# The last four steps of a two-level Winograd graph kernel, finished product by product and in pieces of 128 features

## The chip, the cores and the metric

The kernel runs on one core of one Trainium2 chip. The metric is device microseconds of one execution, the median of a few runs. Engines are named as in the profile: PE (TensorE matmul) and PEld (its weight loads), DVE (VectorE), ACT (ScalarE), POOL (GpSimd), SP (SyncE, which issues DMAs here). Places in time are microseconds from the start of the profiled span.

## What is computed

Two graph layers over N = 4096 nodes with D = 512 features, all float32:

```python
# layer 0: inc = adj + (adj > 0) / row norm of that mask
x1  = layernorm(x + (inc @ x) / rowsum(inc))
# layer 1: A2 = adj + I, dscale = diag(A2) ** -0.5
temp = A2 @ x1 @ W.T
out  = layernorm(x1 + relu((dscale[:, None] * A2 * dscale[None, :]) @ temp))
```

The three 4096 x 4096 products are what costs time. The change touches the last of them and the relu, the addition of x1 and the layernorm behind it.

## The kernel before

**Tiling.** Each product is done with Winograd's form of Strassen's method, seven products in place of eight, at two levels in layer 1. The outer level gives seven operand pairs p (1 to 7); the inner level gives, for each pair, seven matmuls. `steps` (L189) lists the work of layer 1: k is 2 for A2 @ x1 and 3 for the normalised product, s (0, 1) a half of the output nodes, p in the order of ORDER (L179), kk (0 to 7) a slice of the contraction. A step is seven matmuls of 128x512 into seven PSUM banks, one for each inner product (`multiply2`, L272 to L278); the banks collect the eight kk of one (k, s, p). bank(7) is the spare one (`spare`), used for transposes. Features lie on partitions in these results, nodes along the free dimension.

**Operands of a step.** `load` fetches a tile `a` of adjacency (four quarters of 512 columns). `prepare` adds the identity where the diagonal lies (`complete`, L174) and forms four sums S3, S1, S2, S4 with DVE in `add_up`: L167 (two sums, 1024 wide), L169 (S2), L170 (S4). `sum_b` (L257 to L259) does the same for the other operand, once for two steps. Steps are prepared LA = 2 ahead.

**After a group of eight steps** `outer` decodes the seven banks into quarter tiles C (`inner`, L684 to L692): quarter 0 is q1+q2; with u2 = q6+q1 and u3 = q7+u2 quarter 1 is q3+(u2+q5), quarter 2 is q4-u3, and quarter 3 is -u3-q5. They are added to or subtracted from what lies in C (L695, L699, L913).

**Rows of the result.** When a half of C is done for some nodes, `layer1` (L859) takes a block of 128 nodes: four 128x128 transposes on PE (L844) into the spare bank, `rectify` on ACT (L848: relu with scale), and in `rest`, one step later, `add` of x1 on DVE (L695), bn_stats (L149), bn_aggr (L151), sqrt on ACT (L153), `normalise` (L159 and L161 on DVE, L162 on ACT) and a store issued by POOL (L873). x1 comes back from DRAM with `fetch` (L857, POOL queue). Sixteen blocks of s = 0 and eight of s = 1 go this way, one or two beside each step.

**The last eight blocks** (h = 1, s = 1) need the very last group, k = 3, s = 1, p = 4. Their second halves of features (H = 256 wide) are done early by `layer1_first`: two blocks at a time, two transposes each into bank 7, rectify into o[:, H:D], x1 added by POOL (L887), bn_stats (L892). These are taken up from `queue` beside the steps of the last group, two for each of its steps as long as there are any. In the last group three layer1 blocks and then four layer1_first pairs remain, so the fourth pair comes by itself at step kk = 4.

**The end.** The last TAIL = 3 steps (kk = 5, 6, 7) are prepared but not multiplied in the loop. `finish` (L895 on) does them product by product, all three steps of q1, then of q2, q6, q5, q3, q7, q4 (L908), so that quarters are decoded while later products run. c21 holds four quarters of 128 features by 512 nodes: c21[:, 0] and c21[:, 1] belong to blocks 0 to 3 (r = 0), c21[:, 2] and c21[:, 3] to blocks 4 to 7 (r = 1). `put` (L910 to L913) makes a quarter in two DVE operations: the sum into a temporary y, then y - c21. `turn(t)` transposes both quarters' columns of block t into a bank of its own, rectifies 256 features, and adds x1 on POOL (L922). `measure(t)` is bn_stats, bn_aggr, sqrt (L927, L929, L931); `leave(t)` normalises on ACT or, in one tensor_scalar, on DVE (L940, L941), and stores through SP (L942). The order is written out by hand:

```python
        multiply(q7)
        for t in range(4):
            turn(t)
        ... u3, put(3) ...
        multiply(q4)
        measure(0); measure(1)
        put(2, ...)
        for t in range(4, 8):
            turn(t)
        ... measure and leave, alternating ...
```

**What sets the order.** The scheduler is off (`manual_schedule`): every engine runs its instructions in the order in which the program issues them, and waits on semaphores. So an instruction that waits holds all that stands behind it on its engine, DMA issues on POOL and SP included.

Of the kernel before, what the change touches and what calls it, by code (L numbers as in the profile page):

```python
# [8 lines left out]
F32 = mybir.dt.float32  # L9
# [4 lines left out]
P = 128  # L14
# [12 lines left out]
def tile_adj_resnorm_d2(  # L27
# [148 lines left out]

    TAIL = 3
    LA = 2
# [49 lines left out]
    def prepare(n):  # L228
        k, s, p, kk = steps[n]
        for i in range(n, len(steps) if n == len(steps) - TAIL else n + 1):  # L230
            complete(i)
# [8 lines left out]
        made["s"] += 1  # L240
        sm = (work, pools["work"], work)[i % 3].tile([P, 4, SW], F32, tag="s", name="s")
        add_up(sm, a)
# [616 lines left out]
    def layer1(h, item):  # L859

        j, r, cols = item
        b = j + h * NP
        y = late.pop(b)
        o = late["pool"].tile([P, D], F32, name="o", bufs=4)
        ps = spare()
        turn_back(ps, 0, h, r, cols, (0, 1))
        rectify(o, ps, b)

        def rest():
            add(o, y)  # L870
            mv, sd = statistics([o])
            normalise(o, mv, sd)
            nc.gpsimd.dma_start(out=out[b * P:(b + 1) * P, :], in_=o)  # L873
        later.append(rest)

    def layer1_first(h, *items):
# [4 lines left out]
        for i, (j, r, cols) in enumerate(items):  # L881
            b = j + h * NP
            o = late["pool"].tile([P, D], F32, name=f"o{b}")
            st = late["pool"].tile([P, 2, 6], F32, name=f"st{b}")
            rectify(o[:, H:D], ps[:, i * H:(i + 1) * H], b)
# [3 lines left out]
        def rest():  # L889
            for j, _, _ in items:  # L890
                _, o, st = late[j + h * NP]
                nc.vector.bn_stats(st[:, 1, :], o[:, H:D])  # L892
        later.append(rest)

    def finish(h, items, acc):  # L895


        c21 = C_of[3][h][0]
        q1, q2, q6, q5, q7, q3, q4 = range(7)
        p1, p5, u2, u3 = (row_tile(t, 1) for t in ("p1", "p5", "u2", "u3"))  # L900
        w2 = row_tile("t", 1, (P, 4, H))[:, 0:2, :].rearrange("p a d -> p (a d)")
        tail = [(steps[n][3], factors(n)) for n in range(len(steps) - TAIL, len(steps))]
        stats = {}

        def multiply(m):
            for kk, f in tail:
                right, left = f[m]
                nc.tensor.matmul(acc[m], left, right, start=False, stop=(kk == NQ - 1))  # L908

        def put(i, op):  # L910
            y = row_tile("y", 2)
            op(y)
            nc.vector.tensor_sub(c21[:, i, :], y, c21[:, i, :])  # L913

        def turn(t):
            j, r, cols = items[t]
            b = j + h * NP
            ps = bank((t + 7) % 8)
            turn_back(ps, 0, h, r, cols, (0,))
            y, o, _ = late[b]  # L920
            rectify(o[:, 0:H], ps[:, 0:H], b)
            nc.gpsimd.tensor_add(o[:, 0:H], o[:, 0:H], y[:, 0:H])  # L922

        def measure(t):
            b = items[t][0] + h * NP
            _, o, st = late[b]
            nc.vector.bn_stats(st[:, 0, :], o[:, 0:H])  # L927
            mv = late["pool"].tile([P, 2], F32, name=f"mv{b}")
            nc.vector.bn_aggr(mv, st)  # L929
            sd = late["pool"].tile([P, 1], F32, name=f"sd{b}")  # L930
            nc.scalar.activation(sd, mv[:, 1:2], AF.Sqrt, bias=eps_t)  # L931
            stats[b] = mv, sd

        def leave(t, by_act):
            b = items[t][0] + h * NP
            o, (mv, sd) = late[b][1], stats[b]
            if by_act:
                normalise(o, mv, sd)
            else:
                nc.vector.reciprocal(sd, sd)  # L940
                nc.vector.tensor_scalar(o, o, mv[:, 0:1], sd, op0=ALU.subtract, op1=ALU.mult)  # L941
            nc.sync.dma_start(out=out[b * P:(b + 1) * P, :], in_=o)  # L942

        multiply(q1)
        nc.scalar.copy(p1, acc[q1])
        multiply(q2)
        put(0, lambda o: nc.vector.tensor_add(o, acc[q2], p1))
        multiply(q6)
        nc.vector.tensor_add(u2, acc[q6], p1)
        multiply(q5)  # L950
        nc.scalar.copy(p5, acc[q5])
        nc.vector.tensor_add(w2, u2, p5)
        multiply(q3)
        put(1, lambda o: nc.vector.tensor_add(o, acc[q3], w2))
        multiply(q7)
        for t in range(4):
            turn(t)
        nc.vector.tensor_add(u3, acc[q7], u2)
        put(3, lambda o: nc.vector.scalar_tensor_tensor(o, u3, -1.0, p5, op0=ALU.mult, op1=ALU.subtract))
        multiply(q4)  # L960
        measure(0)
        measure(1)
        put(2, lambda o: nc.vector.tensor_sub(o, acc[q4], u3))
        for t in range(4, 8):
            turn(t)
        measure(2)
        measure(3)
        leave(0, True)
        leave(1, False)
        leave(2, True)  # L970
        measure(4)
        leave(3, False)
        measure(5)
        leave(4, True)
        measure(6)
        leave(5, True)
        measure(7)
        leave(6, True)
        leave(7, False)

# [117 lines left out]
```

## Time and profile before

| | |
|---|---|
| median of 3 runs | 2285.16 us (2283.39 to 2285.18) |
| the profiled execution's own time | 2284.03 us |
| its span, first to last instruction | 2282.1 us |
| PE busy | 2255.1 us, 99% |
| DVE busy | 1854.4 us, 81% |
| ACT busy | 417.3 us, 18% |
| POOL busy | 383.3 us, 17% |
| mean granted TensorE clock | 0.998 |

The page gives the busy time and share of each engine, the busy share in 40 slices of the span, the DMA queues, the chain of work that ended last (followed back from the last instruction to what released each step), and the costliest groups of instructions by line, engine and shape. A line number like L908 is one of the kernel before, unless the text says otherwise. A timeline row reads: start, duration, engine, line, operation, output<-inputs, shapes, count, and in brackets how long the engine was idle before it and what released it.

### The profile page before, as it was taken

How to read it: one execution, taken by the hardware profiler on the slowest of the kernel's cores; microseconds unless marked ns; L12 is line 12 of the kernel's file. 1: busy time of each engine (PE TensorE's matmuls, PEld its weight loads, DVE VectorE, ACT ScalarE, POOL GpSimd, SP SyncE). 2: the span in 40 equal slices, each digit the busy share in tenths (PEclk: the TensorE clock that was granted, in tenths of full speed). 3: DMA queues.
4: the chain of work that ended last, by engine and by line, in shares of the span. 5: the costliest groups of instructions: out<-in, count | busy, mean ns of one | idle time of the engine just before them, and what ended most of it. 6: DMA issues, size and time to landing. Idle time of an engine off the chain costs nothing.

```text
span 2282.1 us, 22004 instructions
## 1 busy us (share of the span) xinstructions
PE 2255.1 (99%) x7359; PEld 1380.3 (60%) x7359; DVE 1854.4 (81%) x2619; ACT 417.3 (18%) x991; POOL 383.3 (17%) x548
## 2 busy tenths in 40 slices
PE   8999999999999999999999999999999999999997
PEld 6888888888888844444555444555544444444443
DVE  6988988988988777788876778887666788776788
ACT  4333223332232000000222100122110011100013
POOL 0111112211111110001333300232320000100013
PEclk9999999999999999999999999999999999999999
DMA  9788777878777576575767857576785676766573
GB/s 330 274 287 262 260 233 270 272 262 270 238 240 239 187 266 259 198 283 184 270 240 227 262 209 271 191 283 261 209 256 218 220 258 241 253 238 227 209 269 117
DMA packets 155936, 555.80 MB, mean 244 GB/s; under 512 B 17920, under 2 KB 32272, under 8 KB 117424
## 3 DMA queue, kind: packets, MB, share of 16 engines
q1 hardware_dynamic: 114624, 417.38, 51.6%
q0 software_dynamic: 41200, 137.03, 18.2%
q8 instruction: 58, 0.95, 0.2%
q14 instruction: 54, 0.44, 0.1%
HBM read 434.78 MB, written 119.55 MB: 243 GB/s over the span
## 4 chain that ended last, share of the span: by engine, by line
PE 89%; DVE 5%; DMA 3%; ACT 2%; issue 1%; POOL 0%; SPq 0%; DVEq 0%; ACTq 0%
PE q L278 55%; PE q L472 27%; PE q L766 3%; PE q L485 2%; DMA nat<-adj 2%; DVE s L167 1%; PE q L908 1%; PE q L844 1%; DVE s L169 0%; ACT z L816 0%; ACT nat L332 0%; DVE a L442 0%; DVE mask L435 0%; ACT t L816 0%; DVE ts L257 0%
## 5 line engine op out<-in xcount | busy, mean ns | idle before, releaser
L278 PE MATMUL q<-s,ts 128*128 128x512 f32 x1326 | 612.2, 592 | 0.1
L472 PE MATMUL q<-b,s 128*128 128x256 f32 (+1 forms) x1920 | 454.4, 379 | 0.0
L278 PEld LDWEIGHTS q<-s,ts 128*128 128x128 f32 x1326 | 251.6, 190 | 299.1 <-issue 268.3
L167 DVE TENSOR_TENSOR s<-a 128x1024 f32<-128x1024 f32 x236 | 290.2, 1230 | 161.4 <-PE q L278 131.3
L472 PEld LDWEIGHTS q<-b,s 128*128 128x128 f32 x1920 | 363.1, 189 | 53.1 <-DVE z L510 0.5
L472 PE MATMUL q<-b,a 128*128 128x258 f32 (+1 forms) x1440 | 352.5, 380 | 0.7 <-ACT p L503 0.6
L278 PE MATMUL q<-a,tr 128*128 128x512 f32 x692 | 329.4, 592 | 1.8 <-DMA a<-adj_r 1.8
L472 PEld LDWEIGHTS q<-b,a 128*128 128x128 f32 x1440 | 272.5, 189 | 40.9 <-ACT p L503 1.5
L278 PE MATMUL q<-s,tr 128*128 128x512 f32 x442 | 225.7, 592 | 0.0
L278 PEld LDWEIGHTS q<-a,tr 128*128 128x128 f32 x692 | 129.5, 190 | 145.1 <-issue 138.9
L332 ACT ACTIVATE nat<-nat,tiny 128x512 f32<-128x512 f32 x240 | 170.9, 714 | 235.9 <-DMA nat<-adj 235.7
L278 PE MATMUL q<-a,ts 128*128 128x512 f32 x346 | 176.8, 592 | 0.0
L169 DVE TENSOR_TENSOR s<-a,s 128x512 f32<-128x512 f32 x236 | 167.7, 711 | 8.1
L170 DVE TENSOR_TENSOR s<-a,s 128x512 f32<-128x512 f32 x236 | 167.3, 709 | 8.0
L442 DVE TENSOR_TENSOR a<-a,mask 128x1024 f32<-128x1024 f32 x123 | 150.7, 1225 | 6.6 <-DVE mask L435 0.5
L435 DVE SCALAR_TENSOR_TENSOR mask<-a,sc 128x1024 f32<-128x1024 f32 (+2 forms) x129 | 154.1, 1196 | 2.1
L278 PEld LDWEIGHTS q<-s,tr 128*128 128x128 f32 x442 | 84.0, 190 | 92.1 <-issue 84.6
L684 ACT COPY p<-q 128x512 f32<-128x512 f32 x27 | 15.6, 577 | 631.5 <-PE q L278 631.5
L278 PEld LDWEIGHTS q<-a,ts 128*128 128x128 f32 x346 | 65.7, 190 | 83.0 <-issue 76.1
L425 POOL DMA_DIRECT2D oa<-sr x64 | 57.7, 902 | 283.8 <-DVE sr L416 181.6
L873 POOL DMA_DIRECT2D out<-o x24 | 13.1, 547 | 507.8 <-ACT o L162 507.8
L278 PE MATMUL q<-r,tr 128*128 128x512 f32 x192 | 92.7, 593 | 0.0
(193 smaller groups left out, 2129.4 us busy)
## 6 DMA issues: line engine op xcount, KB each, us to landing
a<-adj_r SPq DMA_DIRECT2D x112, 1024.0 KB, 6.6
a<-oa SPq DMA_DIRECT2D x80, 1024.0 KB, 5.3
nat<-adj SPq DMA_DIRECT2D x240, 256.0 KB, 7.4
a<-adj_q SPq DMA_DIRECT2D x60, 1024.0 KB, 6.2
tr<-ob SPq DMA_DIRECT2D x112, 512.0 KB, 4.0
oa<-sr POOLq DMA_DIRECT2D x64, 512.0 KB, 7.2
oa<-r POOLq DMA_DIRECT2D x32, 1024.0 KB, 9.2
y<-x POOLq DMA_DIRECT2D x64, 256.0 KB, 7.2
```

The costliest lines, as they stand in the source:

```text
L167: nc.vector.tensor_add(s[:, S3:S1 + 1, :], a[:, A11:A22 + 1, :], a[:, A21, :].unsqueeze(1).to_broadcast([P, 2, w]))
L169: nc.vector.tensor_add(s[:, S2, :], a[:, A11, :], s[:, S1, :])
L170: nc.vector.tensor_add(s[:, S4, :], a[:, A12, :], s[:, S2, :])
L278: nc.tensor.matmul(acc[m], left, right, start=(kk == 0), stop=(kk == NQ - 1))
L332: nc.scalar.activation(y, a, AF.Sign, bias=tiny, scale=2.0 ** 64, accum_out=accum)
L425: nc.gpsimd.dma_start(out=dst, in_=sr.rearrange("p m (k i) -> p (m k) i", i=P))
L435: nc.vector.scalar_tensor_tensor(m, v, 0.0, s.unsqueeze(1).to_broadcast(list(v.shape)), op0=ALU.is_gt, op1=ALU.mult)
L442: nc.vector.tensor_add(z, z, y)
L472: nc.tensor.matmul(acc[m][:, 0:w], left, b[:, right, 0:w], start=(kk == 0), stop=(kk == NP - 1))
L485: nc.tensor.matmul(y[:, 0:w], left, slots[kk][:, op, 0:w], start=(kk == 0 and left is k1), stop=(kk == NP - 1 and left is k2))
L766: nc.tensor.matmul(ps, left[:, e, :], wt[:, right, e, :], start=(e == 0), stop=(e == 1))
L844: nc.tensor.transpose(ps[:, at + i * P:at + (i + 1) * P], C_of[3][h][d // 2][:, 2 * r + d % 2, cols], ident)
```

## The change

TAIL is 4: the steps kk = 4 to 7 of the last group are done by `finish`, and the sums of the last two go into tiles of the half that is finished (C_of[3][0]). In `layer1` x1 is added by GpSimd, directly behind the rectify. In `finish` each quarter is prepared so that one operation decodes it after its last product: e0 = p1 - c21[0], then c21[0] = q2 + e0, and so on. Blocks 0 to 3 are turned behind the first of q7's four products, each with its x1 added by DVE or GpSimd in turn, its statistics and its sqrt. Blocks 4 to 7 are done in two pieces of 128 features: one from c21[3], ahead of the last product of q4, and one from c21[2], whose subtraction is done in four parts of 128 columns. Their statistics come from four pieces, also in layer1_first. Two of the first four blocks are normalised by GpSimd.

```diff
--- before.py
+++ after.py
@@ -174,7 +174,7 @@
         nc.vector.tensor_add(pair, pair, ident.unsqueeze(1).to_broadcast([P, 2, P]))
 
 
-    TAIL = 3
+    TAIL = 4
     LA = 2
     ORDER = {2: (4, 5, 1, 6, 7, 2, 3), 3: (2, 3, 5, 1, 6, 7, 4)}
 
@@ -227,7 +227,7 @@
 
     def prepare(n):
         k, s, p, kk = steps[n]
-        for i in range(n, len(steps) if n == len(steps) - TAIL else n + 1):
+        for i in range(n, len(steps) if n == len(steps) - TAIL + 1 else n + 1):
             complete(i)
         a = loaded.pop(n, None)
         r = resident[kk] if k == 2 and p != 4 and p != 7 else None
@@ -238,7 +238,11 @@
             a = r
         i = made["s"]
         made["s"] += 1
-        sm = (work, pools["work"], work)[i % 3].tile([P, 4, SW], F32, tag="s", name="s")
+        if n < len(steps) - 2:
+            sm = (work, pools["work"], work)[i % 3].tile([P, 4, SW], F32, tag="s", name="s")
+        else:
+
+            sm = C_of[3][0][n - len(steps) + 2]
         add_up(sm, a)
         if k == 2 and p in (1, 2) and kk < EARLY:
             raises.append(lambda: nc.vector.tensor_add(r, r, a))
@@ -865,9 +869,9 @@
         ps = spare()
         turn_back(ps, 0, h, r, cols, (0, 1))
         rectify(o, ps, b)
+        nc.gpsimd.tensor_add(o, o, y)
 
         def rest():
-            add(o, y)
             mv, sd = statistics([o])
             normalise(o, mv, sd)
             nc.gpsimd.dma_start(out=out[b * P:(b + 1) * P, :], in_=o)
@@ -881,102 +885,122 @@
         for i, (j, r, cols) in enumerate(items):
             b = j + h * NP
             o = late["pool"].tile([P, D], F32, name=f"o{b}")
-            st = late["pool"].tile([P, 2, 6], F32, name=f"st{b}")
+            st = late["pool"].tile([P, 2 + 2 * r, 6], F32, name=f"st{b}")
             rectify(o[:, H:D], ps[:, i * H:(i + 1) * H], b)
             y, late[b] = late[b], (late[b], o, st)
             nc.gpsimd.tensor_add(o[:, H:D], o[:, H:D], y[:, H:D])
 
         def rest():
-            for j, _, _ in items:
+            for j, r, _ in items:
                 _, o, st = late[j + h * NP]
-                nc.vector.bn_stats(st[:, 1, :], o[:, H:D])
+
+                w = H // (1 + r)
+                for i in range(H // w, D // w):
+                    nc.vector.bn_stats(st[:, i, :], o[:, i * w:(i + 1) * w])
         later.append(rest)
 
     def finish(h, items, acc):
+
 
 
         c21 = C_of[3][h][0]
         q1, q2, q6, q5, q7, q3, q4 = range(7)
         p1, p5, u2, u3 = (row_tile(t, 1) for t in ("p1", "p5", "u2", "u3"))
-        w2 = row_tile("t", 1, (P, 4, H))[:, 0:2, :].rearrange("p a d -> p (a d)")
+        e0, e1 = row_tile("y", 2), row_tile("y", 2)
         tail = [(steps[n][3], factors(n)) for n in range(len(steps) - TAIL, len(steps))]
         stats = {}
 
-        def multiply(m):
-            for kk, f in tail:
+        def multiply(m, of=slice(0, TAIL)):
+            for kk, f in tail[of]:
                 right, left = f[m]
                 nc.tensor.matmul(acc[m], left, right, start=False, stop=(kk == NQ - 1))
 
-        def put(i, op):
-            y = row_tile("y", 2)
-            op(y)
-            nc.vector.tensor_sub(c21[:, i, :], y, c21[:, i, :])
-
-        def turn(t):
-            j, r, cols = items[t]
-            b = j + h * NP
-            ps = bank((t + 7) % 8)
-            turn_back(ps, 0, h, r, cols, (0,))
+        def piece(t, f, ps, add_up):
+
+            b = items[t][0] + h * NP
             y, o, _ = late[b]
-            rectify(o[:, 0:H], ps[:, 0:H], b)
-            nc.gpsimd.tensor_add(o[:, 0:H], o[:, 0:H], y[:, 0:H])
-
-        def measure(t):
+            rectify(o[:, f], ps, b)
+            add_up.tensor_add(o[:, f], o[:, f], y[:, f])
+
+        def turn(t, i, ps, at):
+
+            _, r, cols = items[t]
+            nc.tensor.transpose(ps[:, at:at + P], c21[:, 2 * r + i, cols], ident)
+
+        def measure(t, i, w):
             b = items[t][0] + h * NP
             _, o, st = late[b]
-            nc.vector.bn_stats(st[:, 0, :], o[:, 0:H])
+            nc.vector.bn_stats(st[:, i, :], o[:, i * w:(i + 1) * w])
+
+        def deviation(t):
+            b = items[t][0] + h * NP
             mv = late["pool"].tile([P, 2], F32, name=f"mv{b}")
-            nc.vector.bn_aggr(mv, st)
+            nc.vector.bn_aggr(mv, late[b][2])
             sd = late["pool"].tile([P, 1], F32, name=f"sd{b}")
             nc.scalar.activation(sd, mv[:, 1:2], AF.Sqrt, bias=eps_t)
-            stats[b] = mv, sd
-
-        def leave(t, by_act):
+            stats[t] = mv, sd
+
+        def leave(t, by=None):
             b = items[t][0] + h * NP
-            o, (mv, sd) = late[b][1], stats[b]
-            if by_act:
+            o, (mv, sd) = late[b][1], stats[t]
+            if by is None:
                 normalise(o, mv, sd)
             else:
                 nc.vector.reciprocal(sd, sd)
-                nc.vector.tensor_scalar(o, o, mv[:, 0:1], sd, op0=ALU.subtract, op1=ALU.mult)
+                by.tensor_scalar(o, o, mv[:, 0:1], sd, op0=ALU.subtract, op1=ALU.mult)
             nc.sync.dma_start(out=out[b * P:(b + 1) * P, :], in_=o)
 
         multiply(q1)
         nc.scalar.copy(p1, acc[q1])
+        nc.vector.tensor_sub(e0, p1, c21[:, 0, :])
         multiply(q2)
-        put(0, lambda o: nc.vector.tensor_add(o, acc[q2], p1))
+        nc.vector.tensor_add(c21[:, 0, :], acc[q2], e0)
         multiply(q6)
         nc.vector.tensor_add(u2, acc[q6], p1)
+        nc.vector.tensor_sub(e1, u2, c21[:, 1, :])
         multiply(q5)
         nc.scalar.copy(p5, acc[q5])
-        nc.vector.tensor_add(w2, u2, p5)
+        nc.vector.tensor_add(e1, e1, p5)
+        nc.vector.tensor_add(c21[:, 3, :], c21[:, 3, :], p5)
         multiply(q3)
-        put(1, lambda o: nc.vector.tensor_add(o, acc[q3], w2))
-        multiply(q7)
+        nc.vector.tensor_add(c21[:, 1, :], acc[q3], e1)
+        multiply(q7, slice(0, 1))
         for t in range(4):
-            turn(t)
+            ps = bank((7, 0, 1, 2)[t])
+            for i in range(2):
+                turn(t, i, ps, i * P)
+            piece(t, slice(0, H), ps[:, 0:H], (nc.vector, nc.gpsimd)[t % 2])
+            measure(t, 0, H)
+            deviation(t)
+        multiply(q7, slice(1, TAIL))
         nc.vector.tensor_add(u3, acc[q7], u2)
-        put(3, lambda o: nc.vector.scalar_tensor_tensor(o, u3, -1.0, p5, op0=ALU.mult, op1=ALU.subtract))
-        multiply(q4)
-        measure(0)
-        measure(1)
-        put(2, lambda o: nc.vector.tensor_sub(o, acc[q4], u3))
+        nc.vector.scalar_tensor_tensor(c21[:, 3, :], u3, -1.0, c21[:, 3, :], op0=ALU.mult, op1=ALU.subtract)
+        nc.vector.tensor_add(c21[:, 2, :], c21[:, 2, :], u3)
+        multiply(q4, slice(0, TAIL - 1))
+        leave(0, nc.gpsimd)
+        leave(1)
+        ps = bank(3)
         for t in range(4, 8):
-            turn(t)
-        measure(2)
-        measure(3)
-        leave(0, True)
-        leave(1, False)
-        leave(2, True)
-        measure(4)
-        leave(3, False)
-        measure(5)
-        leave(4, True)
-        measure(6)
-        leave(5, True)
-        measure(7)
-        leave(6, True)
-        leave(7, False)
+            turn(t, 1, ps, (t - 4) * P)
+        for t in range(4, 8):
+            piece(t, slice(P, H), ps[:, (t - 4) * P:(t - 3) * P], nc.gpsimd)
+        multiply(q4, slice(TAIL - 1, TAIL))
+        leave(2)
+        leave(3, nc.gpsimd)
+        for t in range(4, 8):
+            measure(t, 1, P)
+        for t in range(4, 8):
+            cols = items[t][2]
+            nc.vector.tensor_sub(c21[:, 2, cols], acc[q4][:, cols], c21[:, 2, cols])
+            ps = bank((5, 7, 0, 1)[t - 4])
+            turn(t, 0, ps, 0)
+            piece(t, slice(0, P), ps[:, 0:P], nc.gpsimd)
+        for t in range(4, 8):
+            measure(t, 0, P)
+            deviation(t)
+            if t > 4:
+                leave(t - 1, (None, nc.vector)[t % 2])
+        leave(7)
 
     def take_up(item):
         kind, args = item
```

## The prediction

> **What bounds the kernel now.** I read the page first (busy shares, then the chain that ended last), then the timeline of the last 50 us for each engine. The page:
>
> ```profile
> span 2282.1 us, 22004 instructions
> ...
> PE 2255.1 (99%) x7359; PEld 1380.3 (60%) x7359; DVE 1854.4 (81%) x2619; ACT 417.3 (18%) x991; POOL 383.3 (17%) x548
> ...
> PE 89%; DVE 5%; DMA 3%; ACT 2%; issue 1%; POOL 0%; SPq 0%; DVEq 0%; ACTq 0%
> ```
>
> PE is the bound up to its last product. A product (128x512) shows as two MATMUL records 0.43 us apart, so 0.86 us; a step's seven take 6.0 us. The change deletes no product and no transpose, so it can win only behind the last product, and lose only by making PE wait. The end of the chain in order of time:
>
> ```profile
> 2249.05 0.44 PE q L844 x4
> 2249.49 15.45 PE q L908 x36
> ...
> 2268.81 0.56 DVE y L963
> 2269.37 0.02 issue
> 2269.40 0.69 DVE c L913
> ...
> 2277.73 0.55 DVE o L941
> ```
>
> The reader is to see that finish() (L908) keeps PE busy without a hole, and that some 9.9 us of DVE, ACT and GpSimd work follow the last product (2268.39, the end of the last L908 group in the timeline) until the last normalise ends at 2278.28. 3.82 us more (the last store, the closing barrier) end the span at 2282.1. DVE in the 20 us before:
>
> ```profile
> 2246.22 4.72 POOL L887 TENSOR_TENSOR o<-o,y 128x256 f32<-128x256 f32 x4 [1.96 <-DMA y<-x]
> ...
> 2246.90 1.21 DVE L167 TENSOR_TENSOR s<-a 128x1024 f32<-128x1024 f32 x1
> ...
> 2248.14 1.10 DVE L169 TENSOR_TENSOR s<-a,s 128x512 f32<-128x512 f32 x1
> ...
> 2249.27 1.10 DVE L170 TENSOR_TENSOR s<-a,s 128x512 f32<-128x512 f32 x1
> ...
> 2254.89 0.69 DVE L169 TENSOR_TENSOR s<-a,s 128x512 f32<-128x512 f32 x1
> ...
> 2255.62 1.10 DVE L170 TENSOR_TENSOR s<-a,s 128x512 f32<-128x512 f32 x1
> 2255.76 0.19 PEld L908 LDWEIGHTS q<-s,ts 128*128 128x128 f32 x1 [0.24 <-DVE s L169]
> ```
>
> Two things. DVE is busy back to back here, and the S2 sum of the last step (L169, ends 2255.58) comes barely before PE needs it: the load at 2255.76 is released by it. And the same L169 takes 0.69 us alone but 1.10 while a GpSimd add runs: DVE operations with two SBUF sources and GpSimd adds exclude each other. Held part: 1.10-0.69 plus a 0.03 joint, 0.44 us of a 256-wide add's 0.72 (the pair at 2236.75: 1.41 for two).
>
> **1. Four deferred steps (TAIL 4).** Before, the seven products of step 4 stood between the third and fourth layer1_first transposes, and the tail held 21. Now the fourth transposes follow the third on PE at once, both in bank 7, so they wait for two rectifies (L848 x2, 0.84 us, and latencies): 1.2 us. Above all the tail runs product by product: the q6 product of the last step, which needs the S2 sum, comes after eight q1/q2 and three q6 products. Transposes at 2242.44 (as before), two times 0.44, 11 x 0.858: PE is there at 2252.75. Before it was there at 2256.19. With DVE where it is now (2255.58) PE would wait 2.8 us, wherever the wait shows (bank 7 or S2). So DVE is the gate, unless it gets 2.8 us faster. The S buffers of the last two steps move into the finished quarter, whose readers (L844 up to 2232) are long done: no wait.
>
> **2. GpSimd adds x1 in layer1.** DVE loses three 512-wide adds ahead of that sum (L695 at 2235.83, 2238.10, 2243.97): -3 x 0.73 = -2.2. The statistics of two-piece blocks grow: eight bn_stats stand ahead instead of six (four of 128, 0.27 from the line through 0.41 at 256 and 0.69 at 512): +0.2. Against it: a 512-wide GpSimd add has no row; its hold lies between 0.44 (as at 256) and 0.88 (twice that); I take 0.88. The first falls behind the rectify that ends at 2226.2, onto the 2048-wide L699 at 2226.41: about 0.95. The second, behind the rectify at 2229.35, onto L169: 0.85. The third needs an x1 load that now stands on GpSimd's queue behind the second add (before it went out at 2213.8); it lands about 4 us later, near 2235.9, and this add and the two 256-wide ones run in a row against L257 to L259: 1.8. With the 1.35 that the four adds at 2246 cost now and still cost: +3.6 of new waits; joints +0.3. Sum -2.2+0.2+3.6+0.3 = +1.9: S2 at 2257.5. Ends: no new wait, -2.0; every hold in full, +2.2. The other twenty-one adds lie in earlier groups, where the page's slices show DVE at 6 to 8 tenths beside a full PE: I cost them at nothing, covered by PE's steps of 6.0 us (uncovered, at most 0.9 each).
>
> The Trainium skill, SBUF — State Buffer, "SBUF: two separate sides", says the shared pair is an exclusive lock held for the whole instruction, and only against DVE operations with two SBUF inputs (or in a 2-port mode). The rows agree on who waits, not on how long: 0.41 us of a 0.72 us add. By the page's rule nine adds ahead of S2 (three of about 1.4, six of 0.72) could hold DVE 8.5 us rather than the 5.3 of the rows, and the sum below would be up to 3.3 us later.
>
> **3. From the gate to the first four blocks.** q6's last product at 2257.6, then nine more (q5, q3, first of q7), 10 x 0.858; transposes and latency 0.45: ACT starts the first rectify at 2266.6.
>
> **4. The loop over blocks 0 to 3 is a chain.** deviation(t) is now inside it, so ACT's order is rectify 0, sqrt 0, rectify 1, ... and ACT works in order: rectify t+1 stands behind a sqrt that waits for DVE. Per block: rectify 0.47, add 0.42 on DVE or 0.72 on GpSimd, bn_stats 0.41, aggregate 0.21, sqrt 0.29, joints 0.1 to 0.15: 1.9 or 2.25. Four, without the last sqrt: 7.9 us. In the trace of before four rectifies take 1.57 together (2265.19) and no sqrt stands between them. DVE's u3 is queued behind measure(3), and for it wait c21[3], four transposes and, behind these on PE, the last product. u3 starts 2274.5, plus 0.69+0.03+0.69: c21[3] at 2275.9. PE would have come there after eight transposes (0.87) and six products (5.15) from 2266.2, at 2272.2: it idles 3.8 us, and the last product ends near 2277.5.
>
> **5. The pieces.** Transposes at 2276.0. ACT does block 1's normalise (0.81, behind DVE's last in-place add) before the rectifies; then 0.36 (rectify of 128 columns, from 0.48 at 256 and 0.69 at 512), four GpSimd adds of 128 (0.5, then 0.46 each: between 0.35 and 0.72 by the 256 row), bn_stats 0.27: 4.1 us until DVE, in order, reaches the four quarter subtractions: 2280.1, 2.6 us after the last product.
>
> **6. The end.** From there: subtract 0.29, transpose 0.4, rectify 0.36, first add, 1.7 to the first bn_stats; four rounds of bn_stats, aggregate and reciprocal, two DVE normalises (0.55) and two nb, 4.1; last ACT normalise 0.84: 6.6 us instead of 9.9. This is the gain of the small pieces, 3.3 us. The one-operation decode takes one 0.69 us operation off each quarter; for q4 it is in the 6.6, the others lie beside products and count nothing (uncovered: 0.7 each). Last operation at 2286.7. The stores are less bunched: 3.6 instead of 3.82. Span 2290.3; the execution's time lies 1.9 over its span (2284.03 to 2282.1): **2292.2**, 8.2 over its own time. The median of the runs, 2285.16, is 1.1 above the profiled one, so I leave it at 2292.
>
> A GpSimd tensor_scalar of 512 has no row of that size. It lies between 0.3 (the 128x32 row, L656) and 3.0 (twice the 1.50 mean of the dearest 256-wide group, L773). I take 0.9, near two uncontended holds. Up to 1.4 each of the two hides behind ACT's work; above, each delays the round of adds behind it: 2.1 us more at 2.5, 3.2 at 3.0.
>
> **Rivals.**
> A. *The port costs nothing*: the new adds fall between DVE operations that do not need it. For: the bn_stats rows (0.41) do not stretch beside GpSimd. Against: L699 and L257 to L259 have two SBUF sources. PE's bank-7 wait then sets the pace: -3.6, 2288.6.
> B. *Not slower: the chain is hidden.* If blocks 0 to 3 take 4.1 us instead of 7.9 (ACT not held by the sqrts), c21[3] is ready as PE comes, the 3.8 us wait goes and all behind it moves: 2288.4, within 0.2%. Above 4.1 each us counts. For: the 1.57 of four rectifies. Against: the order on ACT.
> C. *GpSimd is dearer*: a tensor_scalar of 2.5 gives 2294.3, of 3.0 2295.4. For: its two-source adds cost 1.7 times DVE's (0.72 to 0.42). Against: it has one tensor source.
> D. *All covers hold* (A, B, and the 2.6 of step 5): 2282.2.
>
> **Chances.** Forecast 0.62, A 0.12, B 0.08, C 0.12, D 0.06 (it lies 0.13% below the median; half of it is counted as faster). 0.2% is 4.6 us, about what this kernel's measurement can tell from no change; slower begins at 2289.7. Faster 0.03; within 0.23 (A, B, half of D); slower 0.74 (forecast and C). The range goes from just below A and B to C's end: 2287.5 to 2295.5.
>
> **What would show it.** The last PE records in the timeline: a hole of 1 us or more before the fourth layer1_first transposes, the load for the last S2 released by DVE and near 2257.5, a hole near 4 us before the transposes of c21[3], one near 2 to 3 before the last four. ACT with rectify and sqrt alternating about every 2 us; L703 (L699 before) at 3.2 instead of 2.28. From first quarter subtraction to last operation 6.6. It is wrong if ACT's four rectifies stand together, if DVE's adds do not stretch, or if an earlier group shows PE holes.

## The result, and the profile after

The changed kernel takes 2294.64 us, the median of 6 runs (2292.94 to 2295.53), beside 2284.95 us for the kernel before on the same chip (6 runs, 2283.18 to 2287.24). That is 9.7 us more; the ratio is 1.0043, with a 95% interval of 1.003 to 1.0055. The forecast was slower, 2292.0, with a range of 2287.5 to 2295.5. The profiled execution took 2295.49 us, its span is 2293.4, its clock 0.996.

Lines of the changed kernel carry numbers 4 above those of the kernel before up to the row functions (L848 for L844, L852 for L848, L703 for L699); the new places in finish are L916 (the products), L923 (x1 added to a piece), L928 (transposes), L933, L938 and L940 (bn_stats, bn_aggr, sqrt), L950 (a normalise in one tensor_scalar), L976 to L978 (u3, c21[3], c21[2]) and L994 (the quarter subtractions).

The page after, in the three lines that were shown of before:

```profile
span 2293.4 us, 22018 instructions
...
PE 2257.6 (98%) x7358; PEld 1380.7 (60%) x7359; DVE 1859.2 (81%) x2606; ACT 417.9 (18%) x994; POOL 419.3 (18%) x576
...
PE 88%; DVE 6%; DMA 3%; ACT 1%; issue 1%; POOL 0%; SPq 0%; DVEq 0%; ACTq 0%
```

PE is as full as it was (2257.6 us busy for 2255.1), and the span is 11.3 us longer. So time has come in as holes on PE; behind its last product the span has even become 1.6 us shorter (12.1 us from 2281.26, 13.7 from 2268.39 before). POOL has grown by 36 us, the adds and the two normalises that it took over; DVE has lost the adds of layer1 and one of its three normalises of the last blocks (the other came from ACT) and has yet grown by 4.8. PE's timeline has the holes, in brackets:

```profile
2246.69 0.66 PE L848 MATMUL q<-ident,c 128*128 128x128 f32 x4 [1.50 <-ACT o L852]
2248.28 0.66 PE L848 MATMUL q<-ident,c 128*128 128x128 f32 x4 [0.93 <-ACT o L852]
...
2260.02 1.13 PE L916 MATMUL q<-c,ts 128*128 128x512 f32 x2 [1.64 <-DVE c L169]
...
2278.47 1.09 PE L928 MATMUL q<-ident,c 128*128 128x128 f32 x4 [3.53 <-DVE c L977]
2279.35 1.91 PE L916 MATMUL q<-a,ts 128*128 128x512 f32 x2
2283.49 1.16 PE L928 MATMUL q<-ident,c 128*128 128x128 f32 x4 [2.23 <-DVE c L994]
```

In the same part, the last 60 us, the kernel before had only one hole above 0.3 us, ahead of its last transposes:

```profile
2270.24 1.06 PE L844 MATMUL q<-ident,c 128*128 128x128 f32 x8 [1.85 <-DVE c L913]
```

(Ahead of this part both kernels have eight such holes each, one of 1.83 us before and 1.97 after among them.) The reader is to see who releases them: ACT's rectifies twice, the S2 sum (L169) once, then u3's chain (L977), then the quarter subtraction (L994). The five sum to 9.8 us.

**A measure of the end alone.** Executions of every kernel here differ by some microseconds in their first part, which the change doesn't touch: the first of ACT's 27 copies of p (L684, L688 with four lines more) starts between 847.0 and 852.3. So beside each time I give the *stretch* from the start of the last of these copies to the end of the span. It is 2282.1 - 2212.8 = 69.3 us before and 2293.4 - 2215.5 = 77.9 after: 8.6 us more, all of it in the end of the kernel. It comes from one trace for each kernel; up to a place that their edits leave alone, kernels agree in it to between 0.01 and 0.2 us, so differences of a few tenths are at its edge. To compare places with those of the prediction, 2.7 us (2215.5 - 2212.8) is taken off.

The chain of waits of the last 25 us after, each piece with start, duration, engine and line:

```profile
2269.17 0.48 ACT o L852
...
2270.84 0.29 ACT sd L940
2271.13 0.37 ACT o L852
...
2273.03 0.29 ACT sd L940
2273.33 0.37 ACT o L852
...
2274.89 0.29 ACT sd L940
2275.18 0.37 ACT o L852
...
2277.04 0.56 DVE u L976
...
2279.18 2.06 POOL o L950
2281.24 1.68 POOL o L923 x4
2282.92 2.05 POOL o L950
2284.97 0.43 POOL o L923
...
2289.42 0.81 ACT o L162
```

Rectify and sqrt take turns on ACT (L852, L940), 1.9 or 2.2 us for each of the four blocks, as step 4 had it. In the kernel before the four rectifies stand together:

```profile
2265.19 1.57 ACT L848 ACTIVATE o<-q,dscale 128x256 f32<-128x256 f32 x4 [4.73 <-PE q L844]
```

Then two pieces of 2.06 us stand in the chain where the forecast had 0.9 each: GpSimd's normalises (L950), with its rows of adds (L923) behind them.

### The profile page after: what moved, and what is told of

Same layout as the page of the kernel before. It is cut to its first block, busy times and chain, and to the rows that moved or that the text cites. A ratio compares the mean times of both kernels' runs of the same rounds, so it can differ in the third digit from the quotient of the medians.

```text
span 2293.4 us, 22018 instructions
## 1 busy us (share of the span) xinstructions
PE 2257.6 (98%) x7358; PEld 1380.7 (60%) x7359; DVE 1859.2 (81%) x2606; ACT 417.9 (18%) x994; POOL 419.3 (18%) x576
## 4 chain that ended last, share of the span: by engine, by line
PE 88%; DVE 6%; DMA 3%; ACT 1%; issue 1%; POOL 0%; SPq 0%; DVEq 0%; ACTq 0%
PE q L282 52%; PE q L476 31%; PE q L770 3%; DMA nat<-adj 1%; DVE s L167 1%; DMA b<-x 1%; DVE s L169 1%; PE q L489 1%; DVE ts L261 1%; ACT z L820 0%; PE q L848 0%; ACT t L820 0%; DMA a<-adj_r 0%; PE q L916 0%; DVE ts L262 0%
## 5 line engine op out<-in xcount | busy, mean ns | idle before, releaser
L169 DVE TENSOR_TENSOR s<-a,s 128x512 f32<-128x512 f32 x234 | 169.3, 723 | 8.0
L688 ACT COPY p<-q 128x512 f32<-128x512 f32 x27 | 15.5, 576 | 630.4 <-PE q L282 630.4
L872 POOL TENSOR_TENSOR o<-o,y 128x512 f32<-128x512 f32 x24 | 34.2, 1426 | 446.6 <-ACT o L852 443.6
L261 DVE TENSOR_TENSOR ts<-tr 128x512 f32<-128x512 f32 x112 | 87.1, 778 | 7.5 <-DMA tr<-ob 7.5
```

Of the source, the lines that this page charges most:

```text
L169: nc.vector.tensor_add(s[:, S2, :], a[:, A11, :], s[:, S1, :])
L261: nc.vector.tensor_sub(t[:, :, 0:2, :], b[:, :, 0:4:3, :], b[:, :, 1:2, :].to_broadcast([P, 2, 2, P]))
L872: nc.gpsimd.tensor_add(o, o, y)
```

## Experiments

In each pair of numbers the first is the median above that of the kernel before, run beside it, with the ratio's interval, the second the stretch above 69.3.

**1. The adds alone.**

```diff
 rectify(o, ps, b)
+nc.gpsimd.tensor_add(o, o, y)
 def rest():
-    add(o, y)
```

> The kernel before with one part of the change: layer1 adds x1 on GpSimd instead of on DVE, nothing else. My theory (step 2 of the prediction): DVE loses three adds of 0.73 us ahead of the last step's S2 sum, and waits 3.6 us more for the port it shares with GpSimd, so S2 ends near 2257.3 instead of 2255.58 and PE, which needs it at 2256.19, stands still for about 1.5 us; time 1 to 2.5 us above the kernel before. Rival A (the port costs nothing): S2 ends about 2 us earlier than before, PE never waits for it, and the time is that of the kernel before, 0 +- 0.5 us. What tells them apart in the trace: the duration of the 2048-wide DVE decode (L699 in before: 3.2 or 2.28 us) and the idle time of PE before the last S2's loads.

Measured: +2.5 us (1.0001 to 1.0018), stretch +1.8. The timeline of this kernel, whose lines are those of before but for the add, now L868:

```profile
2228.58 3.36 DVE L699 SCALAR_TENSOR_TENSOR c<-c,c 128x2048 f32<-128x2048 f32 x1
...
2233.10 1.65 DVE L169 TENSOR_TENSOR s<-a,s 128x512 f32<-128x512 f32 x1
...
2244.64 0.81 ACT L162 ACTIVATE o<-o,nb,rs 128x512 f32<-128x512 f32 x1 [0.49 <-DVE nb L161]
2245.36 0.82 ACT L848 ACTIVATE o<-q,dscale 128x256 f32<-128x256 f32 x2
...
2246.23 0.66 PE L844 MATMUL q<-ident,c 128*128 128x128 f32 x4 [1.51 <-ACT o L848]
```

The size is that of my theory, and rival A falls: the 2048-wide decode takes 3.36 us (2.28 before), L169 1.65 (0.69 alone). The place isn't: PE has no hole ahead of the last S2, but one of 1.51 us before the third layer1_first pair. DVE's delay reaches ACT first: its normalise (L162) waits for nb from the late DVE, the rectify of the second pair stands behind that on ACT (2245.36), and bank 7 is free only then.

**2. TAIL 4 alone.**

```diff
-TAIL = 3
+TAIL = 4
-... if n == len(steps) - TAIL else n + 1
+... if n == len(steps) - TAIL + 1 else n + 1
+sm of the last two steps: C_of[3][0][n - len(steps) + 2]
```

> The kernel before with TAIL 4 alone (the last four steps product by product, their two last S buffers in the finished quarter); finish and layer1 as before. My theory (steps 1 and 3): the fourth pair's transposes wait about 1.2 us for bank 7, then PE reaches the last step's q6 before DVE has made its S2, and has ten products behind this gate instead of seven: 2.5 to 3.5 us above the kernel before, with two holes on PE, one of about 1 us ahead of the fourth layer1_first pair, one of 1.5 to 2.8 us ahead of the last S2's loads. Rival (the deferral is free, as PE only does the same products in another order): no hole above 0.3 us, time within 0.5 us of the kernel before.

Measured: +3.6 us (1.0009 to 1.0028), just above the range, stretch +3.0, inside it. Its PE timeline has both holes at the places and in the sizes that were expected:

```profile
2243.63 0.66 PE L848 MATMUL q<-ident,c 128*128 128x128 f32 x4 [0.93 <-ACT o L852]
...
2255.61 1.12 PE L912 MATMUL q<-c,ts 128*128 128x512 f32 x2 [1.88 <-DVE c L169]
```

**3. The new finish alone.** The edit is the opposite: TAIL 3 and its two companions, and `add(o, y)` in `rest`, with the changed finish kept.

> The changed kernel with TAIL 3 and with layer1's x1 adds back on DVE, that is the kernel before with the new finish alone (decode in one operation, deviation inside the loop over blocks 0 to 3, blocks 4 to 7 in pieces of 128, two normalises on GpSimd). My theory (steps 4 to 6, with the GpSimd normalise at the 2.07 us that the profile after shows): the loop is a chain on ACT of 7.9 us, so PE stands still 3 to 4 us before the transposes of the second half of blocks 4 to 7, the GpSimd rounds of adds are 1 to 2 us late, and the end from the first quarter subtraction takes 7 instead of 9.9 us; sum 5 to 7 us above the kernel before. Rival B (the chain is hidden, the loss of the change comes from the tail and the port): at most 2 us above the kernel before, or below it by up to 2.

Measured: +5.3 us (1.0016 to 1.0034), stretch +5.9. The hole ahead of c21[3]'s transposes is 5.25 us, larger than the 3 to 4 expected and than the changed kernel's 3.53: with TAIL 3 two products fewer (one of q7, one of q4, 0.86 us each) stand on PE beside the chain, and the chain is as long. The rival falls. The three parts alone sum to 1.8 + 3.0 + 5.9 = 10.7 us of stretch, together they cost 8.6: some of the waits cover each other.

**4. Three repairs at once.**

```diff
     measure(t, 0, H)
-    deviation(t)
+for t in range(4):
+    deviation(t)
-nc.gpsimd.tensor_add(o, o, y)       # and add(o, y) back in rest()
-leave(0, nc.gpsimd)
+leave(0)
-leave(3, nc.gpsimd)
+leave(3)
```

> The changed kernel with three repairs and TAIL 4 kept: deviation(t) in a loop of its own behind the four measures, layer1's x1 adds back on DVE, and the normalises of blocks 0 and 3 on ACT instead of GpSimd. My theory: the chain, the port and the 2.07 us GpSimd operation account for 5 to 6 us of the 9.7 that the change costs; what is left, 3 to 4.5 us above the kernel before, is TAIL 4 (a hole of some 3 us in all on PE before the last S2) and the rest of the new order. ACT's four 256-wide rectifies then stand within 2 us of each other. Rival (the loss sits in TAIL 4 and in the pieces themselves: many small operations on every engine): no more than 2 us of the 9.7 comes back, time 7.5 us or more above the kernel before.

Measured: +2.4 us (1.0001 to 1.0019), stretch +2.3. So 6.3 us of the stretch (7.3 of the medians) come back, slightly more than the 5 to 6 that I expected, and the rival falls. What is left can be seen in the timeline:

```profile
2276.65 1.53 DVE L933 BATCH_NORM_STATS2 st<-o 128x6 f32<-128x128 f32 x4 [1.63 <-POOL o L923]
...
2278.10 0.86 DVE L995 TENSOR_TENSOR c<-q,c 128x128 f32<-128x128 f32 x4
...
2278.43 0.98 PE L928 MATMUL q<-ident,c 128*128 128x128 f32 x4 [3.05 <-DVE c L995]
```

The hole ahead of c21[3]'s transposes is gone, but one of 3.05 us stands before the last four: the last product ended at 2275.37, and the subtractions (L995) come at 2278.10, because the bn_stats of the first pieces (L933) stand ahead of them on DVE and wait 1.63 us for GpSimd's adds.

**5. The chain undone, alone.** Of the diff above only the first three lines.

> The changed kernel with one edit: deviation(t) of blocks 0 to 3 stands in a loop of its own behind the four measures, so that no sqrt stands between two rectifies on ACT. My theory (step 4): the four rectifies take about 1.6 to 2.5 us instead of 6.4, u3 starts 3 to 3.5 us earlier, but the two GpSimd normalises and DVE's own queue keep part of it: 2 to 3 us below the changed kernel (some 6.5 to 7.7 us above the kernel before, where the changed one is 9.7 above). Rival (the chain is only the place where another wait shows: u3 waits for DVE's queue in any order): less than 1 us below the changed kernel. In the trace: the distance between the starts of the first 256-wide rectify and of u3's addition, 7.8 us in the changed kernel; my theory 4 to 5, the rival 6.5 or more.

Measured: +4.0 us (1.0008 to 1.0025), stretch +4.3, so 4.3 us of stretch below the changed kernel: more than the 2 to 3 that I expected.

```profile
2264.74 1.57 ACT L852 ACTIVATE o<-q,dscale 128x256 f32<-128x256 f32 x4 [3.91 <-PE q L928]
...
2268.43 0.63 DVE L977 TENSOR_TENSOR u<-q,u 128x512 f32<-128x512 f32 x1
...
2270.35 0.60 PE L928 MATMUL q<-ident,c 128*128 128x128 f32 x4
...
2274.95 0.98 PE L928 MATMUL q<-ident,c 128*128 128x128 f32 x4 [3.14 <-DVE c L995]
```

The four rectifies stand together (1.57 us), u3 comes 3.7 us behind the first instead of 7.8 (4 to 5 were expected), and the transposes at 2270.35 have no hole before them. This is rival B's condition made true, and its time: B gave 2288.4, measured is 2288.86.

**6. No normalise on GpSimd, alone.** The last four lines of the diff in 4.

> The changed kernel with one edit: the normalises of blocks 0 and 3 go to ACT (0.81 us each) instead of GpSimd (2.08 and 2.06 us in the profile after). Theory C (the dear GpSimd operation): the first delays the four 128-wide adds by about 1.2 us, the second the last four adds by about 0.9; without them 1 to 2 us less than the changed kernel, the distance from the transposes of c21[3] to the first quarter subtraction falls from 4.7 to under 4, and from there to the last operation from 7.1 to 6.6 or less. Rival (ACT is as full as GpSimd: two normalises of 0.81 ahead of the rectifies cost the same): the distance to the first quarter subtraction stays at 4.5 or more and the time within 0.5 us of the changed kernel.

Measured: +8.1 us (1.0022 to 1.0046), stretch +7.8; the interval overlaps with the changed kernel's, so the verdict is the trace's: 0.8 us of stretch. Of this 0.2 us lies ahead of the first rectify, where the edit changes nothing. From the transposes of c21[3] (2276.40) to the first quarter subtraction (2281.00) are 4.6 us, as good as the 4.7 of the changed kernel: there the rival is right, ACT's two normalises (1.52 us) now stand ahead of the four rectifies. From there to the end of the last operation (2287.58) are 6.6 instead of 7.1: there the theory is right, for 0.5 us.

**7. The queues reordered.** Three repairs, TAIL 3, and:

```diff
-leave(0); leave(1)                  # ahead of the first pieces
-leave(2); leave(3)
-for t in range(4, 8): measure(t, 1, P)
 for t in range(4, 8):
     ... the quarter subtractions and the last pieces ...
+leave(0); leave(1); leave(2); leave(3)
+for t in range(4, 8): measure(t, 1, P)
```

> The three repairs of the run before (deviation out of the loop, layer1's adds on DVE, no normalise on GpSimd), TAIL 3, and the quarter subtractions moved on DVE's queue ahead of the normalises of blocks 0 to 3 and of the bn_stats of the first pieces. In the run with three repairs the last product ended 2.7 us before the first quarter subtraction, which stood behind bn_stats that waited for GpSimd's adds. My theory (all that the finish loses, it loses by what stands ahead of it on an in-order queue, not by the work itself): the hole before the last four transposes falls from 3 to about 1 us, and the time is 0 to 1.5 us above the kernel before. Rival (the pieces cost by their number, as every small operation has a fixed part): 2.5 us or more above the kernel before, with DVE busy without a gap from the first quarter subtraction on.

Measured: -0.6 us, no difference that can be told (0.9993 to 1.0010), stretch 0.0. With TAIL 4, the adds in layer1 and GpSimd's normalises taken out and the queues reordered the whole loss is gone, with pieces, quarter subtractions and one-operation decodes kept. The edit also moves ACT's normalises of blocks 0 to 3 behind the pieces; what that part is worth alone wasn't tried. Its PE timeline has these holes, the second 0.39 us where about 1 was expected:

```profile
2268.29 0.63 PE L924 MATMUL q<-ident,c 128*128 128x128 f32 x4 [1.14 <-DVE c L974]
...
2270.16 0.99 PE L924 MATMUL q<-ident,c 128*128 128x128 f32 x4 [0.39 <-DVE c L985]
```

**8. What can be had of the change.**

```diff
 # the kernel before, its decodes in one operation, and
+for t in range(4, 8):
+    c21[:, 2, cols] = acc[q4][:, cols] - c21[:, 2, cols]
     turn(t)                         # 256 features, as before
-leave(1, False); leave(3, False); leave(5, True)
+leave(1, True);  leave(3, True);  leave(5, False)
```

> The kernel before with only what its profile can use: the decode in one operation, the last quarter subtracted in four parts of 128 columns with each part's transposes directly behind it, and normalises 1 and 3 on ACT, 5 on DVE; TAIL 3, the adds, the order of blocks 0 to 3 and the 256-wide rectifies as before. My theory: the first block's transposes start 0.3 us behind the last product instead of 1.4, nothing is late ahead of it, so the end after the last product takes about 9 us instead of 9.9: 0.5 to 1.5 us below the kernel before. Rival (the end is a row of GpSimd adds and DVE statistics, and an earlier start only lengthens its waits): within 0.3 us of the kernel before; or slower, if the normalises 1 and 3 that ACT takes over hold its rectifies.

Measured: -0.6 us (0.9988 to 1.0004), stretch -1.1. In time this isn't told from the kernel before. In the trace it is:

```profile
2270.37 0.83 DVE L969 TENSOR_TENSOR c<-q,c 128x128 f32<-128x128 f32 x4
...
2270.75 1.07 PE L844 MATMUL q<-ident,c 128*128 128x128 f32 x8 [0.73 <-DVE c L969]
...
2277.99 0.81 ACT L162 ACTIVATE o<-o,nb,rs 128x512 f32<-128x512 f32 x1
...
2278.23 0.55 DVE L941 TENSOR_SCALAR o<-o,mv,sd 128x512 f32<-128x512 f32 x1
```

The transposes follow 0.73 us behind the last product (1.85 before; 0.3 was expected), since the first quarter subtraction stands behind a block's statistics on DVE, and from that product's end (2270.02) to the last operation's (2278.80) are 8.8 us instead of 9.9. The edit holds three things, the decodes in one operation, the quarters and who normalises; which of them brings the 1.1 us isn't separated.

**9. Three repairs with TAIL 3**: the repairs of 4, and TAIL 3; the subtractions where the changed kernel has them.

> The three repairs (deviation out of the loop, layer1's adds on DVE, no normalise on GpSimd) with TAIL 3, the quarter subtractions still behind the bn_stats of the first pieces. It stands between two runs that I have: three repairs with TAIL 4, 2.4 us above the kernel before, and TAIL 3 with the quarter subtractions moved ahead, 0.6 below. If the subtractions' place on DVE's queue is what counts: a hole of about 3 us on PE before the last four transposes stays, and the time is 1 to 2 us above the kernel before. If TAIL counts: the hole shrinks by itself, the time is within 0.7 us of the kernel before.

Measured: +1.6 us (1.0000 to 1.0018), stretch +0.9. The hole before the last four transposes stays, so it is the place on DVE's queue, not TAIL, that makes it:

```profile
2272.06 1.16 PE L924 MATMUL q<-ident,c 128*128 128x128 f32 x4 [3.44 <-DVE c L991]
```

The new order of run 7, the subtractions ahead of the statistics and ACT's normalises behind the pieces, took all but 0.39 us of it away and brought 0.9 us of stretch.

**10. The queues reordered, with TAIL 4.**

> The kernel with the quarter subtractions moved ahead and the three repairs, but TAIL 4. TAIL 4 alone cost 3.6 us (3.0 in the stretch from ACT's last copy of p to the end of the trace) on the kernel before. If its price is the gate at the last step's S2 with ten products behind it, it is paid here as well: 1.5 to 3 us above the kernel before, with a hole of 1.4 to 1.9 us before the last S2's loads. If the new order of finish hides it (fewer DVE operations between the products): within 0.7 us of the kernel before.

Measured: +3.6 us (1.0006 to 1.0024), above the 1.5 to 3 expected, stretch +1.8, inside it, with a hole of 1.69 us before the last S2's loads. TAIL 4's price is paid here as well. It is 1.8 us in the stretch here and 3.0 in run 2, so part of it is hidden by the new order.

**11. Pieces in an order that is to leave no hole ahead of them.** As run 7, but all of q7 first, u3 ahead of the statistics of blocks 0 to 3, all their adds on GpSimd, and another engine for four of the eight normalises.

> Pieces of 128 features, TAIL 3, x1 added on DVE in layer1, with nothing ahead of PE's products that makes them wait: all of q7 before the transposes of blocks 0 to 3, u3 before their statistics, the quarter subtractions before the normalises. It tells what the pieces are worth by themselves, beside the run with quarter subtractions and 256-wide pieces (0.6 us below the kernel before, 1.1 in the stretch from ACT's last copy of p to the end of the trace). My theory (a piece of half the width costs more than half on each engine: 0.28 to 0.36 after 0.39 to 0.47 on ACT, 0.42 after 0.72 on GpSimd, 0.29 after 0.43 on DVE): no better than that run, 0 to 1 us below the kernel before. Rival (the small pieces shorten the end): 1.5 to 3 us below the kernel before.

Measured: +0.1 us (0.9995 to 1.0013), stretch -0.6. The products come without a hole, but one stands ahead of the last four transposes, whose subtractions wait on DVE behind statistics that wait for GpSimd's adds:

```profile
2270.79 0.98 PE L924 MATMUL q<-ident,c 128*128 128x128 f32 x4 [1.65 <-DVE c L985]
```

So the hole was moved, not taken away, and the rival isn't settled. What speaks against it: from the last product's end to the last operation's are 8.7 us here, 8.8 in run 7, where the hole is only 0.39, and 8.8 in run 8 with its 256-wide pieces. Narrow pieces with no hole at all weren't tried.

## Why the prediction was right, and where it was off

Direction, mechanism and order of the holes were right; one hole was not forecast, that of 1.50 us ahead of the third layer1_first pair, which in run 1 comes from the adds by way of ACT. Place by place, after minus 2.7 us:

| | forecast | after - 2.7 |
|---|---|---|
| last step's S2 ends | 2257.5 | 2257.3 |
| first rectify of block 0 | 2266.6 | 2266.5 |
| u3 starts | 2274.5 | 2274.3 |
| transposes of c21[3] | 2276.0 | 2275.8 |
| last product ends | 2277.5 | 2278.6 |
| first quarter subtraction | 2280.1 | 2280.5 |
| last operation ends | 2286.7 | 2287.5 |
| span | 2290.3 | 2290.7 |

1. **TAIL 4** (step 1): right. DVE is the gate. PE waits 1.50 + 0.93 + 1.64 = 4.1 us before it; the prediction had 4.75 (2252.75 to 2257.5). The wait shows at three places, two of them at bank 7, as the step allowed.
2. **GpSimd's adds** (step 2): right in the sum. The rows after:

```profile
2229.05 3.35 DVE L703 SCALAR_TENSOR_TENSOR c<-c,c 128x2048 f32<-128x2048 f32 x1
...
2233.57 1.64 DVE L169 TENSOR_TENSOR s<-a,s 128x512 f32<-128x512 f32 x1
...
2239.18 1.59 POOL L872 TENSOR_TENSOR o<-o,y 128x512 f32<-128x512 f32 x1 [2.96 <-DMA y<-x]
...
2239.69 1.37 DVE L262 SCALAR_TENSOR_TENSOR ts<-ts,tr 128x256 f32<-128x256 f32 x1
...
2259.28 0.69 DVE L169 TENSOR_TENSOR c<-a,c 128x512 f32<-128x512 f32 x1
```

L703 holds 1.07 us more (I had 0.95), L169 0.95 (0.85), L262 0.95 and L263 0.41 (1.8 for the three of that group; 1.36), and the third add does wait for x1 (2.96 us). The step's other half failed: the twenty-one earlier adds were costed at nothing. In all four kernels that have them the 20th of ACT's 27 copies comes 0.4 to 0.5 us late against the 19th (52.8 us apart), in the nine others never (52.3). There ACT's sqrt, which waits for DVE's statistics of a layer1 block, starts 2.6 us later than before (1870.86 for 1868.26) where PE's products come 2.2 later, and the copies stand behind that block's normalise on ACT. It is small, but it is one of the prediction's own signs of being wrong, time lost in an earlier group.
3. **The chain on ACT** (step 4): right, 7.8 us for 7.9, and run 5 takes it away alone. It is the largest term.
4. **Pieces** (step 5) and **end** (step 6): 4.7 us for 4.1, and 7.1 for 6.6. The mis-sized term is GpSimd's tensor_scalar: 2.08 and 2.06 us where I had taken 0.9. It is rival C's mechanism, at less than its lowest price of 2.5. My rule that up to 1.4 each hides left 0.7 over, twice; the places miss by 0.6 and 0.5. Run 6, which has no such normalise, shows the second (7.1 falls to 6.6); the first stays there (4.6), because ACT's normalises took the place of GpSimd's, so for the first the cause is read from the chain after (2279.18, then 2281.24) and not shown by a run.
5. **Stores**: 3.2 us behind the last operation instead of 3.6, and this gives 0.4 of those 1.1 us back.

In sum the forecast's 8.2 over its own execution stands beside 8.6 in the stretch, with 0.4 more from the earlier adds. What is left to the 9.7 of the medians lies within their interval (6.9 to 12.6). The 2292.0 itself is only 6.8 above the median of before that I had then (2285.16): it is added up from the profiled execution and was not raised by the 1.1 us between the two.

Two more things weren't in the prediction. That the quarter subtractions stand behind bn_stats that wait for GpSimd was inside my 4.1 us of step 5, but as a cost of the pieces; runs 4, 7 and 9 show that it is one of the order. And the last product ends 1.1 us later than forecast because it and the transposes ahead of it ran at half the clock (below): from the start of these to its end are 2.79 us, in run 6, at full clock, 1.53. What GpSimd's adds in layer1 cost in the changed kernel, all else kept, wasn't tried; run 1 has them on the kernel before.

## What to carry to other kernels

On engines that work in order, look at what stands ahead of the instruction that frees the bound engine: here the sqrts between four rectifies cost about 4 us, and bn_stats that waited ahead of four subtractions made a hole of 3 us on PE, some 1 us of it in the stretch, with the same work in every order. Before you cut a tail into smaller pieces, look at what half a piece costs: here a rectify of 128 columns took 0.36 us for 0.47 at 256, bn_stats about 0.27 for 0.42, a GpSimd add 0.44 for 0.72, and 128-wide pieces brought nothing over 256-wide ones in the orders tried. What could be kept of the change, 256-wide pieces with decodes in one operation and the last subtraction in quarters (run 8), was worth about 1 us in one trace and nothing that the times can tell. Work moved to GpSimd is not free where DVE has no slack: an add beside DVE's two-source operations came back as a wait of 1 us on DVE, and reached PE through ACT.

## What the hardware showed that I had not expected

- **GpSimd's tensor_scalar** (two operations, 128x512, per-partition scalars) took 2.06 to 2.08 us in the three kernels that have it (the changed one, runs 3 and 5). The same normalise took 0.55 on DVE and 0.81 on ACT, and GpSimd's own add of two 128x512 tensors 1.26 (median of 24). Beside it DVE's one-column L161 took 0.59 instead of 0.16. The Trainium skill (GPSIMD Engine Reference, "4.1 Engine selection") has elementwise operations on GpSimd with one input at roughly line rate and those with two about half as fast as on VectorE. The add agrees (1.26 to DVE's 0.69); this tensor_scalar, 3.8 times DVE's 0.55, does not.
- **A 512-wide GpSimd add** held DVE's two-source operations for 0.95 to 1.07 us of its 1.26, a 256-wide one for 0.41 to 0.44 of 0.72. The Trainium skill (SBUF — State Buffer, "SBUF: two separate sides") has the lock held for the whole instruction; these rows show three quarters of it for the wider add and less for the narrower.
- **The clock fell at holes, and also where PE was busy for a third of the time.** Windows of the changed kernel (columns: length, PE busy with its records, granted clock, DMA share, GB/s), whose hole of 3.53 us begins at 2274.94:

```profile
2276.00:2277.00 1.00, 0.00 (x0) 1.00 0.00 0
2277.00:2278.00 1.00, 0.00 (x0) 0.57 0.00 0
2278.00:2279.00 1.00, 0.53 (x3) 0.50 0.00 0
```

The clock fell to a half at about 2277.14, within the hole, and the last product's two records took 1.91 us. Run 6 has a hole of the same length, and its clock fell at two places:

```profile
2246.00:2247.00 1.00, 0.58 (x5) 0.99 0.80 119
...
2248.00:2249.00 1.00, 1.00 (x2) 0.50 0.98 393
...
2250.00:2251.00 1.00, 1.00 (x3) 0.80 0.00 0
...
2276.40 0.63 PE L928 MATMUL q<-ident,c 128*128 128x128 f32 x4 [3.54 <-DVE c L977]
...
2276.00:2277.00 1.00, 0.60 (x5) 1.00 0.00 0
2277.00:2278.00 1.00, 0.94 (x3) 0.85 0.00 0
```

There it was still 1.00 behind the hole, the two records took 1.07 us, and it fell only at about 2277.7. It had been at a half once more, from about 2247.0 to 2250.4, behind the two short holes of layer1_first (1.50 and 0.93 us). The three places of run 6 lie on steps of 3.41 us: 2250.4 is one step behind 2247.0, and 2277.7 is nine. In the 3.41 us ahead of each fall PE was busy for 1.21 us (changed kernel), 1.23 and 1.31 (run 6); behind steps in which it was busy for 1.77 (changed kernel, from 2256.66) and 1.98 (run 6, from 2270.88) the clock stayed at 1.00. The Trainium skill (TensorE: Matmul & The Clock Gate, "What's actually happening") says that the clock halves after at least one idle window of about 3.4 us, and that the window runs freely. The steps agree with the second, and two holes of one length with different outcomes do too. The first is not what these traces show: the windows ahead of the falls were not idle, PE was busy in over a third of each. It cost nothing here: in the changed kernel the last product ended at 2281.26 and the quarter subtractions, which waited for GpSimd's adds, came at 2283.16, and in run 6 PE had no hole at the last S2, which was its gate in the changed kernel.
